# A two-layer graph network in seven-product form: small products of the unit matrix ahead of TensorE's work, new places for the first and last graphs, and a bank of its own for one seed of the last graph

## The chip, the cores and the metric

The kernel runs on one core of one Trainium2 chip. The metric is the device time of one execution in microseconds; the median of three runs is given. TensorE (PE, with its weight loads PEld), VectorE (DVE), ScalarE (ACT), GpSimd (POOL) and SyncE (SP) each work through a queue of their own in order; SP only issues transfers here.

## The reference

64 graphs of 256 nodes with 512 features pass through two layers. Each layer normalises the rows, applies a ReLU, and adds what a graph layer makes of them.

```
# layer 0
h   = max(layernorm(x), 0)
agg = adj @ h / max(rowsum(adj), 1e-6)
x   = x + relu(concat(h, agg) @ W.T)
# layer 1
h  = max(layernorm(x), 0)
Xw = h @ Wv + bv
e  = leaky_relu((Xw @ aw[:512])[None, :] + (Xw @ aw[512:])[:, None] + ab, 0.2)
T  = adj * exp(e);  T = T / (rowsum(T) + 1e-12)
H  = h @ Wk[0] + bk[0] + (T @ h) @ Wk[1] + bk[1] + (T @ T @ h) @ Wk[2] + bk[2]
x  = x + relu(H)
```

Everything is float32.

## The kernel before

**Stages.** Each graph goes through twelve stages: `loads`, `prepare` (the first normalisation, the scaled adjacency `an`, the turning of both), `prepared`, `wide` (h times the weights of layer 0, in 26 products of 128x128 by 128x256), `layer0` (the adjacency's part in seven such products, and `finish`, which adds the result to `x`), `turn1` (the second normalisation, to `h1n`, and the four dot products `z` on DVE that give `sj`), `transition` (T, turned to `tt`), `moved` (sums of blocks of T on the left side, `st`), `once` (T @ h, to `zg`), `inner` (times Wk[2], to `qf`), `turned1` (the load of the turned `h1n`), and `outer` (all three terms of H, and the output). Matrix products are split into 2x2 blocks and done with seven block products in place of eight. The sums of blocks that this needs are made on POOL (`pool_op`, L422; for the first and last graphs some go to DVE, L420), the evictions from PSUM by ACT (`copy`, L471) and DVE (`plus` and `minus`, L474 and L477; the wide stage's own at L652).

**Order.** No scheduler decides the order. Every operation is put down with `add(...)` under the name of its stage, and gets a time from a table: `AT[stage][n] + graph * 38.52`. `emit` sorts by this time, and each engine's queue is the sorted list of its own operations. The time only sets the order: an operation starts when its engine reaches it and its inputs are there. Graphs 0, 1, 2, 62 and 63 have tables of their own (`_0`, `_1`, `_2`, `_late`, `_last`), all others share one. A first table, `first`, and one named `weights` hold the loads and the making of the weights' forms.

**Places that matter below.**

- The transfers at the head are issued by SP in the order of the tables: the four tiles of W of layer 0 (`weights_l0`, L784, 512 KB each, which land in the buffers of `x[2]` to `x[5]`), `x[0]` in two halves (L904), then adjacencies, `x[1]`, and the weights of layer 1 (L828 to L840). At most eight are under way: the ninth waits for the first, and so on.
- `weights_l0` turns W on PE (L796, 32 transposes in eight banks); ACT copies and DVE sums (L812, L814) make 26 forms of it.
- `transition` sends `sj` to DRAM (L686, `ds`) and reads it back into all partitions as `row` (L687). ACT makes the leaky ReLU and the exponential from it, DVE multiplies with the adjacency (L697), ACT scales (L703) and, for graphs 0, 62 and 63, PE turns the result (`flip_on_pe`, L404), after which one copy on DVE and one on ACT (L410) make `tt`.
- `put` turns blocks on DVE (L376) and writes them to DRAM in four transfers (L380); `get` reads them back (L386). `turned1` gets `h1t` this way; POOL's sums for `outer` (`left_of_h`) wait for it.
- `main` works in three banks `p`, `r`, `d`: products 5, 1, 6 and 7 add up in `p`, and DVE takes the seeds of the others out of `p` between them; products 2 and 3 then add to the two halves of `r`, 4 to `d`. For graph 63 (`last` given) the seed of product 3 stays in the upper half of `r`, product 2 works on the lower half, and an ACT copy (L546) then moves the seed to the bank `y`, in which product 3 works. The copy waits for what uses bank `r`.

Of the kernel before, what the change touches and what calls it, by code (L numbers as in the profile page):

```python
# [11 lines left out]
AF = mybir.ActivationFunctionType  # L12
# [3 lines left out]
P = 128  # L16
# [8 lines left out]
WARM = 0  # L25
TURN = 38.52
AT = {
    "first": (-90.93, -53.23, -117.99, -108.94, -110.36, -116.23, -69.23, -51.75, -160.39, -107.21, -61.21, -22.37, -27.53, -12.34, -45.26, -1.78,
        -84.29, -28.27, -93.32, 13.37, -47.15, -20.43, -156.60, -71.50, -119.21, -46.84, -42.27, -129.45, -122.63, -61.71, -52.35, -32.94, -72.67,
        -62.56, -45.91, -151.57, -67.52, -60.72, 2.83, 15.02, -11.78, 19.40, 29.16, -47.95, -25.77, 48.23, -47.81, -32.81, -19.46, -48.89, 7.13,  # L30
        20.41, -32.63, 17.85, 10.53, -123.51, 5.76, 21.86),
    "inner": (105.13, 108.59, 106.23, 109.69, 109.89, 110.76, 112.05, 116.38, 111.97, 114.07, 117.47, 117.50, 122.79, 115.08, 117.06, 118.02, 137.51),
    "inner_0": (104.64, 107.10, 112.63, 109.63, 108.85, 109.21, 114.17, 115.99, 113.73, 110.41, 129.80, 114.72, 119.54, 110.75, 113.34, 116.02,
        129.11),
    "inner_1": (110.70, 112.22, 111.49, 112.47, 113.83, 115.31, 114.08, 115.66, 116.33, 115.18, 129.29, 117.74, 125.91, 116.89, 117.80, 117.56,
        155.03),
    "inner_2": (110.70, 111.20, 111.98, 113.63, 111.78, 114.32, 114.94, 116.88, 115.46, 116.06, 116.42, 116.98, 124.86, 117.74, 119.04, 117.57,
        134.35),
    "inner_last": (336.53, 367.29, 384.59, 334.45, 391.73, 454.67, 522.64, 533.37, 408.60, 470.37, 504.02, 528.93, 492.30, 558.54, 500.07, 537.12,
        580.23),  # L40
    "inner_late": (108.31, 111.76, 110.85, 113.85, 112.13, 112.69, 114.05, 114.68, 123.33, 115.61, 145.82, 118.27, 122.89, 115.88, 119.11, 120.04,
        164.89),
    "layer0": (20.96, 24.01, 34.26, 38.15, 36.30, 37.47, 38.90, 39.56, 40.20, 40.90, 41.49, 42.16, 41.93, 42.79, 43.22, 43.47, 44.25),
    "layer0_0": (43.30, 43.73, 40.76, 63.15, 62.04, 64.91, 63.69, 65.17, 65.45, 66.86, 68.03, 68.37, 68.31, 69.19, 69.32, 68.45, 68.75),
    "layer0_1": (31.27, 36.57, 33.97, 43.43, 46.13, 48.74, 46.62, 49.21, 46.86, 49.66, 48.01, 49.83, 48.25, 48.79, 50.67, 49.93, 50.78),
    "layer0_2": (24.88, 28.19, 23.22, 43.47, 37.98, 37.09, 39.47, 39.22, 40.19, 41.59, 40.57, 42.04, 42.75, 43.10, 41.23, 47.00, 44.33),
    "layer0_last": (50.01, 57.68, 33.91, 60.79, 65.66, 66.71, 68.41, 66.94, 69.01, 68.24, 69.91, 69.27, 70.80, 71.03, 72.73, 71.96, 75.23),
    "layer0_late": (15.20, 21.71, 35.30, 40.31, 42.84, 48.47, 47.89, 49.57, 47.98, 49.76, 48.90, 49.94, 48.91, 50.48, 49.70, 51.70, 50.97),
    "loads": (-59.49, -45.29),
    "loads_2": (-40.12, -36.06),  # L50
    "loads_last": (-58.91, -32.90),
    "loads_late": (-54.89, -85.13),
    "moved": (89.04, 92.46, 93.17, 93.66, 94.15, 98.50),
    "moved_0": (94.08, 96.00, 97.15, 96.58),
    "moved_1": (87.63, 93.34, 94.62, 96.56, 97.69, 105.10),
    "moved_2": (88.68, 91.56, 91.23, 91.84, 96.02, 106.19),
    "moved_last": (139.05, 163.46, 205.96, 169.91),
    "moved_late": (96.66, 97.72, 100.63, 101.15),
    "once": (61.25, 64.00, 75.09, 75.88, 94.29, 95.59, 94.96, 99.41, 98.19, 98.63, 100.80, 101.23, 101.56, 100.30, 105.75, 103.00, 102.97, 103.89,
        106.56, 107.35, 108.14),  # L60
    "once_0": (85.34, 86.38, 98.69, 87.50, 93.62, 98.46, 98.58, 97.73, 98.58, 100.34, 100.69, 102.20, 101.36, 98.56, 103.24, 103.33, 102.27, 102.98,
        104.33, 105.25, 108.42),
    "once_1": (57.59, 69.48, 97.24, 96.50, 95.31, 95.58, 95.01, 99.66, 97.26, 98.27, 100.29, 102.15, 100.46, 102.80, 103.34, 105.40, 106.15, 108.95,
        105.21, 110.88, 111.17),
    "once_2": (63.41, 76.25, 69.81, 96.68, 93.52, 97.13, 93.09, 100.30, 100.95, 102.43, 103.05, 103.30, 102.21, 102.90, 103.59, 109.13, 104.57,
        107.39, 107.54, 109.97, 115.46),
    "once_last": (102.80, 135.83, 148.28, 162.89, 124.41, 120.18, 145.98, 187.50, 162.35, 203.89, 212.10, 233.57, 187.89, 213.05, 223.02, 232.11,
        256.18, 243.42, 255.25, 267.18, 321.27),
    "once_late": (66.99, 88.23, 64.29, 90.92, 99.96, 101.37, 100.45, 101.19, 101.37, 101.90, 105.80, 107.13, 110.31, 103.81, 110.60, 107.37, 105.93,
        106.50, 106.70, 107.63, 115.35),  # L70
    "outer": (108.93, 110.52, 122.87, 129.37, 114.22, 117.68, 119.41, 120.07, 120.70, 121.57, 122.87, 123.53, 124.60, 125.46, 126.33, 126.99, 127.62,
        130.65, 131.52, 132.19, 128.92, 131.95, 134.55, 134.99, 141.93, 152.31, 138.02, 140.19, 162.69, 160.60, 164.14, 164.93),
    "outer_0": (94.35, 98.74, 125.62, 106.70, 102.31, 116.27, 117.12, 118.24, 117.50, 117.80, 121.31, 124.46, 124.00, 125.58, 126.52, 126.71, 128.22,
        128.87, 132.65, 133.67, 128.80, 131.21, 134.36, 137.61, 140.55, 144.44, 136.33, 141.49, 160.49, 160.36, 163.66, 166.03),
    "outer_1": (106.89, 111.90, 118.77, 120.53, 108.75, 117.68, 119.18, 119.21, 120.59, 120.95, 123.23, 122.93, 123.75, 126.63, 126.70, 127.43,
        127.87, 128.74, 130.19, 132.33, 130.44, 131.84, 139.05, 141.13, 148.79, 152.10, 133.45, 136.68, 160.29, 160.80, 164.22, 166.72),
    "outer_2": (108.39, 111.96, 127.91, 140.81, 108.40, 121.23, 123.19, 121.63, 124.71, 125.64, 126.27, 125.65, 128.28, 128.68, 129.01, 128.91,
        131.04, 134.92, 135.36, 134.36, 132.23, 135.69, 137.94, 142.17, 143.69, 152.32, 138.41, 140.22, 150.30, 161.80, 164.00, 171.57),
    "outer_last": (498.02, 668.57, 694.33, 671.17, 577.46, 581.61, 593.26, 565.87, 615.19, 623.17, 650.49, 630.60, 695.13, 726.44, 735.87, 784.68,
        743.01, 838.42, 843.34, 796.04, 842.17, 761.60, 792.50, 751.08, 788.70, 811.00, 818.37, 858.45, 840.44, 876.17, 953.80, 975.74, 975.14,  # L80
        1020.56, 876.63, 891.60, 907.44, 875.80, 872.80),
    "outer_late": (109.06, 117.31, 186.73, 151.51, 116.15, 116.30, 119.62, 120.47, 120.01, 120.90, 123.12, 123.38, 129.10, 132.52, 132.66, 129.78,
        134.77, 139.77, 140.44, 139.50, 141.87, 144.49, 145.13, 158.57, 188.07, 200.85, 150.49, 152.04, 158.47, 232.29, 199.18, 211.96),
    "prepare": (-43.06, -41.74, -40.72, -35.30, -36.24, -28.72, -27.19, -23.45, -19.80, -15.93, -24.36, -24.98, -20.94, -12.75, -1.76, -2.28, -14.82,
        -13.49, -12.68, -12.13, -11.03, -11.58, -0.32, 1.04, 0.48, 2.14, 1.59),
    "prepare_0": (-84.88, -53.30, -37.93, -28.72, -22.39, -78.13, -74.85, -6.63, -18.20, -7.49, -144.71, -60.68, -137.04, -101.76, -12.58, -21.22,
        -26.38, -2.11, -10.47, 18.05),
    "prepare_1": (-15.07, -17.62, -8.06, -6.13, -0.14, -1.19, -0.63, 0.54, 7.75, 18.63, -38.44, -18.61, -14.54, 4.73, 16.46, 7.28, 12.55, 17.02,
        21.02, 19.33),
    "prepare_2": (-29.75, -29.48, -28.24, -24.75, -27.62, -28.40, -18.19, -16.40, -14.88, -13.91, -13.33, -6.35, -3.17, 8.62, 7.51, 7.67, -7.58,  # L90
        -2.32, -3.08, -1.25, 10.97, -0.12, 9.45, 9.24, 6.13),
    "prepare_last": (-41.49, -47.42, -40.82, -36.74, -38.40, -39.37, -36.21, -27.41, -24.96, -22.93, -7.95, -5.29, -3.53, 0.52, -2.38, -0.41, -8.95,
        -8.06, 0.10, 9.16, 6.05, -3.83, 2.64, 1.68, 2.00, -1.88, -3.02),
    "prepare_late": (-34.61, -47.32, -24.01, -19.75, -22.44, -22.19, -20.22, -19.93, -12.10, -16.22, -28.31, -35.76, -26.99, -25.62, -0.63, -19.64,
        -11.10, -13.45, -13.43, -9.03, -11.19, -7.53, -0.35, -0.68, -1.43, -1.97, 0.33),
    "prepared": (-7.18, 5.89, 11.28),
    "prepared_0": (8.94, 11.22, 28.01, 44.28),
    "prepared_1": (30.89, 31.47, 31.46, 30.86),
    "prepared_2": (13.00, 25.59),
    "prepared_last": (9.25, 6.90, 2.69),  # L100
    "prepared_late": (-3.13, 0.63, 10.23),
    "transition": (52.39, 56.28, 64.51, 63.42, 65.05, 63.97, 66.52, 67.12, 67.73, 68.04, 68.40, 68.92, 69.51, 71.25, 71.80, 70.70, 72.35),
    "transition_0": (74.09, 74.94, 85.61, 86.74, 87.55, 87.22, 90.49, 90.24, 90.60, 91.41, 91.25, 92.03, 91.61, 91.53, 93.51, 94.10),
    "transition_1": (53.67, 62.32, 65.20, 65.85, 69.15, 70.70, 67.77, 67.85, 67.92, 69.48, 74.55, 74.24, 70.13, 70.67, 70.52, 71.81, 77.46),
# [5 lines left out]
    "turn1_1": (49.63, 49.70, 50.51, 51.10, 51.13, 51.73, 53.03, 53.21, 53.66, 53.93, 58.29, 58.86, 64.81, 54.56, 54.30, 58.29, 62.00, 58.02, 61.54),  # L110
    "turn1_2": (43.11, 45.01, 43.93, 52.82, 53.16, 53.50, 49.16, 51.40, 52.03, 52.20, 54.30, 57.90, 58.08, 51.29, 54.09, 59.58, 56.28, 52.52, 56.97),
    "turn1_last": (75.41, 78.96, 77.17, 178.47, 184.64, 192.21, 86.15, 103.27, 80.59, 81.84, 83.21, 85.38, 104.79, 93.44, 122.16, 115.84, 150.29,
        115.69, 113.30),
    "turn1_late": (42.12, 48.32, 51.63, 53.75, 53.93, 54.07, 55.81, 56.33, 52.09, 61.66, 67.71, 71.29, 74.60, 66.82, 79.34, 84.95, 89.16, 79.81,
        97.48),
    "turned1": (100.59,),
# [859 lines left out]
```

## Time and profile before

| | us |
|---|---|
| median of three runs (2547.05 to 2548.68) | 2547.44 |
| the profiled execution | 2545.75 |
| its span | 2544.0 |
| PE busy in the span | 2509.1 (99%) |
| POOL / DVE / ACT busy | 1560.1 / 1653.6 / 1322.6 |
| PE busy in the first 120 us | 95.3 |
| PE busy from 300 to 2300 us | 2000.0 |
| PE busy in the last 144 us | 134.2 |

All times of the profile are microseconds from the start of the span. One line of a timeline gives start, duration, engine, source line, operation, output and input by the names of the program, the number of instructions, and in brackets the idle time before it and what ended that. A product of 128x256 appears as two MATMUL records; at the full clock it takes 0.43 us, a transpose 0.11 us. The column PEclk of a table by stretches is the granted clock of TensorE, 1.00 for the full one. The ends of matmuls are modelled, so a stretch that shows PE busy throughout may hold short waits.

### The profile page before, as it was taken

How to read it: one execution, taken by the hardware profiler on the slowest of the kernel's cores; microseconds unless marked ns; L12 is line 12 of the kernel's file. 1: busy time of each engine (PE TensorE's matmuls, PEld its weight loads, DVE VectorE, ACT ScalarE, POOL GpSimd, SP SyncE). 2: the span in 40 equal slices, each digit the busy share in tenths (PEclk: the TensorE clock that was granted, in tenths of full speed). 3: DMA queues.
4: the chain of work that ended last, by engine and by line, in shares of the span. 5: the costliest groups of instructions: out<-in, count | busy, mean ns of one | idle time of the engine just before them, and what ended most of it. 6: DMA issues, size and time to landing. Idle time of an engine off the chain costs nothing.

```text
span 2544.0 us, 39950 instructions
## 1 busy us (share of the span) xinstructions
PE 2509.1 (99%) x12412; PEld 2213.5 (87%) x12412; DVE 1653.6 (65%) x4099; ACT 1322.6 (52%) x3551; POOL 1560.1 (61%) x2475
## 2 busy tenths in 40 slices
PE   7899999999999999999999999999999999999998
PEld 5688888888888888888888888888888888888887
DVE  5766666666666666666666666666666666666654
ACT  7455555555555555555555555555555555555521
POOL 5565666666666666666666656656666666666640
PEclk9999999999999999999999999999999999999999
DMA  4354454454454454444444544544544544544421
GB/s 150 85 131 117 113 129 120 115 125 117 117 129 112 115 135 110 119 125 120 120 120 116 127 121 111 128 122 113 127 119 117 126 113 116 135 112 115 110 71 44
DMA packets 574571, 296.85 MB, mean 117 GB/s; under 512 B 417171, under 2 KB 540819, under 8 KB 574358
## 3 DMA queue, kind: packets, MB, share of 16 engines
q1 hardware_dynamic: 574358, 294.31, 47.0%
q8 instruction: 98, 1.61, 0.3%
q14 instruction: 115, 0.94, 0.1%
HBM read 162.80 MB, written 131.40 MB: 116 GB/s over the span
## 4 chain that ended last, share of the span: by engine, by line
PE 96%; DVE 1%; DMA 1%; SPq 0%; ACT 0%; issue 0%; POOL 0%; DVEq 0%; ACTq 0%; POOLq 0%
PE bank L459 96%; DMA dh<-turned 0%; DMA x<-in_L_gnn_W_dram 0%; DMA l<-in_L_gnn_Wv_dram 0%; SPq L380 0%; DVE bank L474 0%; DVE zg L420 0%; DMA out_dram<-x 0%; DVE z L677 0%; DVE turned L376 0%; PE bank L404 0%; ACT h1n L362 0%; DVE bank L652 0%; SPq L345 0%; DVE zg L474 0%
## 5 line engine op out<-in xcount | busy, mean ns | idle before, releaser
L459 PE MATMUL bank<-l,s 128*128 128x256 f32 x3292 | 876.9, 380 | 6.6 <-ACT bank L546 2.1
L459 PEld LDWEIGHTS bank<-l,s 128*128 128x128 f32 x3292 | 611.6, 191 | 91.4 <-issue 5.1
L471 ACT COPY stg<-bank 128x256 f32<-128x256 f32 x944 | 337.2, 371 | 524.8 <-PE bank L459 203.6
L459 PE MATMUL bank<-l,zg 128*128 128x256 f32 x1820 | 469.2, 380 | 1.6 <-ACT mz L471 0.9
L459 PE MATMUL bank<-lq,zg 128*128 128x256 f32 x1792 | 447.8, 380 | 3.7 <-DVE zg L474 1.3
L459 PEld LDWEIGHTS bank<-lq,zg 128*128 128x128 f32 x1792 | 340.4, 190 | 51.1 <-DVE zg L474 2.3
L459 PEld LDWEIGHTS bank<-l,zg 128*128 128x128 f32 x1820 | 337.2, 191 | 42.3 <-ACT mz L471 1.7
L422 POOL TENSOR_TENSOR zg<-zg 128x256 f32<-128x256 f32 x183 | 131.7, 733 | 353.8 <-ACT zg L471 347.4
L652 DVE TENSOR_TENSOR bank<-bank,stg 128x256 f32<-128x256 f32 x505 | 210.3, 428 | 202.1 <-PE bank L459 138.8
L459 PE MATMUL bank<-l,h0t 128*128 128x256 f32 x1008 | 291.3, 382 | 1.6 <-DVE q L652 0.8
L422 POOL TENSOR_TENSOR s<-h0t,s 128x256 f32<-128x256 f32 x315 | 234.0, 743 | 0.5
L459 PEld LDWEIGHTS bank<-l,h0t 128*128 128x128 f32 x1008 | 197.4, 197 | 26.8 <-DVE q L652 2.3
L677 DVE SCALAR_TENSOR_TENSOR z<-h1n,v_sb 128x512 f32<-128x512 f32 x256 | 211.9, 828 | 13.1 <-ACT h1n L368 4.4
L459 PE MATMUL bank<-l,h1t 128*128 128x256 f32 x784 | 203.3, 381 | 1.3 <-DVE lo L477 1.0
L471 ACT COPY qf<-bank 128x256 f32<-128x256 f32 x128 | 47.6, 372 | 285.3 <-DVE qf L474 250.3
L422 POOL TENSOR_TENSOR qf<-qf 128x256 f32<-128x256 f32 x122 | 113.5, 930 | 117.4 <-DVE qf L474 117.4
L459 PEld LDWEIGHTS bank<-l,h1t 128*128 128x128 f32 x784 | 153.1, 197 | 20.1 <-DVE lo L477 2.3
L563 DVE SCALAR_TENSOR_TENSOR x<-bank,x 128x512 f32<-128x512 f32 x254 | 165.4, 686 | 2.7 <-PE bank L459 1.9
L459 PE MATMUL bank<-q,sa 128*128 128x256 f32 x512 | 152.9, 380 | 2.3 <-DVE bank L474 1.6
L459 PE MATMUL bank<-qf,st 128*128 128x256 f32 x512 | 152.6, 380 | 0.8 <-DVE qf L420 0.7
L422 POOL TENSOR_TENSOR s<-h0t 128x256 f32<-128x256 f32 x189 | 143.5, 773 | 9.3 <-ACT h0t L410 6.6
L422 POOL TENSOR_TENSOR hf<-h1n,hf 128x256 f32<-128x256 f32 x124 | 91.3, 736 | 89.9 <-PE bank L459 89.9
(178 smaller groups left out, 4418.3 us busy)
## 6 DMA issues: line engine op xcount, KB each, us to landing
dh<-turned SPq DMA_DIRECT2D x500, 128.0 KB, 3.3
h1t<-dh SPq DMA_DIRECT2D x64, 512.0 KB, 3.8
x<-in_x_dram SPq DMA_DIRECT2D x63, 512.0 KB, 4.6
out_dram<-x SPq DMA_DIRECT2D x63, 512.0 KB, 3.1
h0t<-dh SPq DMA_DIRECT2D x61, 512.0 KB, 4.0
a<-in_adj_dram SPq DMA_DIRECT2D x64, 256.0 KB, 4.3
dan<-turneda SPq DMA_DIRECT2D x248, 64.0 KB, 1.9
raw<-dan SPq DMA_DIRECT2D x62, 256.0 KB, 2.7
```

Source lines behind the costliest of these rows:

```text
L422: add("POOL", cost, lambda: getattr(nc.gpsimd, f)(to, p, q), reads, writes)
L459: nc.tensor.matmul(ps, lhs, rhs, start=start, stop=True, skip_group_check=True)
L471: add("ACT", 0.37, lambda: nc.scalar.copy(dst, bank[b][:, cols]), [f"bank{b}"], dkeys)
L563: add("DVE", 0.75 if sums else 0.69, lambda c=c: nc.vector.scalar_tensor_tensor(t[:, c, :], bank[banks[1 + c]], 0.0, t[:, c, :], op0=ALU.m ...
L652: add("DVE", 0.43, lambda f=f, to=to, x=x, y=y: getattr(nc.vector, f)(to, x, y), pbk + [k], tok)
L677: add("DVE", 0.79, lambda s=s, c=c: nc.vector.scalar_tensor_tensor(scr.rearrange("p c n -> p (c n)"), h[:, c, :], 1.0, v_sb[:, s, :], op0= ...
```

## The change

1. `WARM` goes from 0 to 7. `warm` is now called inside `first`, under a table of its own: 7 groups of four products of the unit matrix with itself (128x128 by 128x128) into bank 2, which nothing reads. Their times place five groups at the head of PE's queue, ahead of the first transposes of W, and two groups between the first 12 and the next 16 of these transposes. They need only `ident`, which POOL makes.
2. In `main`, for graph 63, the seed of product 3 goes into a bank of its own (bank 7, lower half) straight from `p`. The ACT copy between products 2 and 3 is gone; both work on different banks.
3. The tables of the first three and last two graphs, and those of `first` and `weights`, get new times. The tables of graphs 3 to 61 stay.
4. Three cost figures of `add` change (0.66 to 0.82, 0.74 to 0.91, 0.45 to 0.61); `emit` does not use them.

What the new times move on the queues, as far as it is spoken of below:

- SP: `x[1]` is loaded first, before W and `x[0]`; the adjacencies of graphs 0, 2 and 1 come right after W; `l_3` of layer 1 moves to the end of the weights (29th), `aw` from 14th to 23rd, the adjacency of graph 3 behind the first writes of the turned `h1n`. `row` of graph 0 stands directly behind its `ds` (before: behind one write of the turned `h1n`); `row` of graph 1 stands behind `ds`, one write of the turned `an`, the load of `h1t` and three writes (before: the load of `h1t`, the load of `x[4]` and four writes).
- PE: the first two products of `wide` for graph 0 stand ahead of the transposes of Wv (before: the first of them behind four of these). The transposes of T of graph 0 follow the last product of `layer0` of graph 1 directly.
- DVE: the products with the adjacency for T of graph 0 stand ahead of the two additions that finish `layer0` of graph 1 (before: behind them).
- ACT: at the head the sums and squares of `x[0]` come before most of the copies of W's forms.
- POOL: the sum that waits for `h1t` of graph 0 comes behind all of the sums of `once` of graph 0 (before: ahead of some). The sum of weights `l_7` stands ahead of the last two sums of `wide` of graph 0 and of the first of `layer0`'s four.
- At the tail, of the last `outer`: product 2 follows product 7 (before: it stands in the middle of it), then 4 and 3. The second of graph 63's dot products `z` stands behind one subtraction of `outer` of graph 62 (before: ahead of it).

```diff
-WARM = 0
+WARM = 7
 AT = {
+    "warm": (-428.00, -428.00, -428.00, -428.00, -428.00, -302.00, -302.00),
...
         p, r, d = banks[:3]
+        e, cols = (banks[4], lo) if last else (r, hi)
...
         step(6, p, lo, terms)
-        plus(bank[r][:, hi], [f"bank{r}"], p, lo, s12, keys[1:])
+        plus(bank[e][:, cols], [f"bank{e}"], p, lo, s12, keys[1:])
         step(7, p, lo, terms)
         if last:
-            x, y = banks[3:]
+            x = banks[3]
             plus(bank[x][:, lo], [f"bank{x}"], p, lo, s21[:, 1], keys[1:])
             last(1, hi, x, lo)
             plus(bank[d][:, lo], [f"bank{d}"], p, lo, s21[:, 0], keys[:1])
             step(2, r, lo, terms)
-            add("ACT", 0.37, lambda: nc.scalar.copy(bank[y][:, lo], bank[r][:, hi]), [f"bank{r}"], [f"bank{y}"])
             last(0, lo, r, lo)
-            step(3, y, lo, terms)
-            last(0, hi, y, lo)
+            step(3, e, cols, terms)
+            last(0, hi, e, cols)
             step(4, d, lo, terms)
             last(1, lo, d, lo)
...
+    def warm():
+
+        for _ in range(WARM):
+            def run():
+                for k in range(FC):
+                    nc.tensor.matmul(bank[2][:, k * P : (k + 1) * P], ident, ident, start=True, stop=True, skip_group_check=True)
+            add("PE", 0.86, run, ["ident"], ["bank2"])
+
     def first():
...
         add("ACT", 1.3, lambda: nc.scalar.copy(spare, mhalf), ["mhalf"], ["spare"])
+        kept = plan.count
+        plan.stage("warm")
+        warm()
+        plan.stage("first")
+        plan.count = kept
         weights_l0()
         load(0, "a")
         load(1, "x")
         load(1, "a")
```

## The prediction

> **What bounds the kernel now.** I read the page's busy shares first, then a table of stretches, then PE's timeline at both ends, and last what PE waits for there on the other queues.
>
> ```profile
> span 2544.0 us, 39950 instructions
> PE 2509.1 (99%) x12412; PEld 2213.5 (87%) x12412; DVE 1653.6 (65%) x4099; ACT 1322.6 (52%) x3551; POOL 1560.1 (61%) x2475
> ```
>
> PE bounds it. The stretches (length, then busy time and instructions of PE, PEld, DVE, ACT, POOL, then PEclk, DMA share, GB/s) say where PE is not at its best:
>
> ```profile
> 20.00:23.40 3.40, 3.40 (x13) 2.85 (x12) 2.66 (x6) 2.06 (x5) 3.24 (x5) 0.51 1.11 331
> 78.00:88.00 10.00, 6.31 (x21) 4.86 (x21) 8.01 (x21) 3.94 (x9) 1.68 (x3) 0.50 0.34 95
> 300.00:2300.00 2000.00, 2000.00 (x9971) 1782.36 (x9970) 1317.35 (x3272) 1064.02 (x2852) 1272.40 (x2024) 1.00 0.49 120
> ```
>
> The middle is full at the full clock. The change leaves its tables alone, and PE's work stays the same except for 28 small products, so everything is won or lost in the first 126 us and the last 20. In the first 120 us PE idles 120 − 95.3 = 24.7, and it runs at half clock until 23.4 and again from 78 to 88. PE's timeline at the head:
>
> ```profile
> 11.08 4.32 PE L796 MATMUL bank<-ident,x 128*128 128x128 f32 x19 [1.12 <-DMA x<-in_L_gnn_W_dram]
> ...
> 19.86 1.00 PE L459 MATMUL bank<-l,h0t 128*128 128x256 f32 x2
> ...
> 80.77 1.22 PE L459 MATMUL bank<-tt,h1n 128*128 128x128 f32 x4 [0.46 <-ACT tt L410]
> ...
> 94.00 1.13 PE L459 MATMUL bank<-lq,zg 128*128 128x256 f32 x4 [0.48 <-DVE zg L474]
> ```
>
> The landmarks of graph 0 are the first product of `wide` (19.86), `once` (80.77) and `inner` (94.00). Between `layer0` of graph 1 (last product about 73.6) and `inner`, PE mostly waits for graph 0's chain, because no other graph has work yet. On SP, DVE and POOL that chain reads:
>
> ```profile
> 57.78 0.35 SPq L686 DMA_DIRECT2D ds<-sj  x1
> 63.50 0.35 SPq L380 DMA_DIRECT2D dh<-turned  x1
> 63.94 0.44 SPq L687 DMA_DIRECT2D row<-ds  x1
> ```
>
> ```profile
> 74.41 0.42 DVE L697 SCALAR_TENSOR_TENSOR z<-z,a 128x256 f32<-128x256 f32 x1
> ```
>
> ```profile
> 89.22 0.84 POOL L422 TENSOR_TENSOR s<-h1t 128x256 f32<-128x256 f32 x1 [9.55 <-DMA h1t<-dh]
> ```
>
> SP sends `row` 6.2 us after `ds`, held behind one write that waits for DVE. DVE reaches the adjacency products at 74.41, though the exponential is ready at 70.6, because the additions at L563 stand ahead. POOL sits 9.55 us behind a sum that needs the turned `h1t`, with sums for `once` queued behind it. The tail, by the chain of waits and by PE's timeline:
>
> ```profile
> 2532.44 0.78 DVE bank L474 x2
> 2533.22 0.02 issue
> 2533.24 0.76 DVE x L756 x2
> ...
> 2534.08 0.37 ACT bank L546
> ```
>
> ```profile
> 2534.49 1.13 PE L459 MATMUL bank<-l,s 128*128 128x256 f32 x4 [2.09 <-ACT bank L546]
> 2535.46 1.82 PE L459 MATMUL bank<-l,h1t 128*128 128x256 f32 x4
> ```
>
> The copy waits for two DVE seeds and two evictions, PE idles 2.09, and the half clock follows: the last ten products (20 records) take 6.29.
>
> **The change part by part** (gains against the profiled 2545.75, which is 1.69 under the median of 2547.44).
>
> *Warm products.* None is in the trace. Records of 128x128 take 0.11 at the full clock (four in 0.45 from 88.53 to 88.98), and twice that at half. A product is two records, so 0.22 or 0.43. The first 20 can start when `ident` is ready, at 1.4 (after two POOL steps of 1.00 and 0.29). If the clock rises as it did before, 3.5 us into steady products (19.86 to 23.4), eight cost 0.43 and twelve 0.22: 3.5 + 2.6, to about 7.5; all at half, to 10.0. What covers this is the load of W. By the transposes' starts, 0.5 MB had landed at 4.35 and 2.75 MB at 11.03, so (11.03 − 4.35)/2.25 = 2.97 us a MB. With `x[1]` now first, W's second tile completes 1.75 MB in, about 8.1, and the group that waited until 11.08 now waits until 11.8 (3.0 MB). The last eight products (1.8) lie inside that wait. So nothing if the clock rises; without cover, 10.0 + 12 × 0.227 + 8 × 0.43 = 16.1 against 11.8, or 4.3 late.
>
> *A. First product of `wide`.* `x[0]`'s second half is 2.0 MB in, 8.8. ACT's sums and squares, now ahead of W's copies, end about 11.4; five small POOL steps take it to 13.0, the two normalisations on ACT to 15.5, and PE's turning with the copies (L410) to 17.15. The product starts at 17.2 instead of 19.86: 2.7. If the clock stays up, part of the 1.8 us lost before 23.4 (half of 3.54) comes back; I take 0.8, as the waits between would fill some of it. A = 3.5, bounds 0 (the loads set it anyway) and 4.5 (2.7 + 1.8).
>
> The row bearing on the clock is the one above: 19 transposes back to back from 11.08 to 15.40 took 4.32/19 = 0.227 each, the spacing of the half clock, and full speed came only 3.5 us after real products began. (PEclk reads 1.00 there, so I go by the spacing.) The Trainium skill, page "TensorE: Matmul & The Clock Gate", section "Part 4: PE-mode transpose", says that transposes don't count as work for the clock; with "Part 1: The HAM clock gate", where an idle window drops it again, the speed won by the warm products would be lost before 17.2, since only transposes lie between. By that rule A would be 2.7 and the sum below 12.6.
>
> *B. Start of `once`.* `row` directly behind `ds` goes out 2.9 after it (the time `ds` needs to be sent and land), 60.7 instead of 63.94: 3.2 earlier. The adjacency products no longer stand behind the additions, worth 3.8 (74.41 − 70.6). Then they end before PE is free, and PE sets the start: `layer0` of graph 1 ends 3.5 earlier, at 70.1, the four turns follow (0.4). The copies to `tt` then stand on ACT behind two evictions of 0.69, 0.2 of small work and two squares of 0.72: 70.5 + 1.4 + 0.2 + 1.4 − 0.4 overlapped + 0.27 = 73.4. `once` at 73.4 against 80.77 is 7.4 in all. Bounds 3.5 (A alone) and 9.5 (copies not held).
>
> *C. `once` to `inner`.* Now 13.2, of which 3.2 is half clock (6.31 busy in 78 to 88) and part POOL's sum for `h1t`; moved behind the sums of `once`, it no longer holds them. What remains is graph 1's chain, whose ACT and DVE work (two L570 0.8, two normalisations 1.45, copies and a normalisation 1.4, then `z` 0.7, turns 1.4, a difference 0.4) ends about 5.0 after `once` starts; four turned products and `zg` with its sums, at the durations of graph 0 before, take 4.6. So 9.6, and `inner` at 83.0: 11.0 in all. Bounds: 13.2 (nothing won) and 5.5 (graph 63's own distance, 2507.34 to 2512.80).
>
> *D. `inner` to graph 1's `once`.* PE idles 3.5 there now (32.0 long, 28.5 of work). Graph 0's sums for `outer` wait for `h1t`, whose DMAs (3.8 in the page's median, 7.6 at most) now start less early than PE arrives. I take −1.0, bounds +3.5 (all idle gone) and −5. The head gives 10.0.
>
> *E. The tail.* Without the copy, and with products 2, 4, 3 behind 7, product 2's 2.2 us cover the 1.2 of DVE seeds. The 2.1 of idle go, and so does the half clock: ten products at full clock take 4.35 + 0.16, so 1.8 more. Against it, graph 63's second `z` stands behind a subtraction of graph 62's `outer` (which waits for PE): about 1.5 late, while `an` was ready at 2504.98 and its turns began at 2505.61, so 0.6 of slack, and some 0.4 of work moved ahead of the turns. I count −0.5. E = 3.4, bounds 1.9 (clock not kept, second wait 0.2) and 4.0.
>
> The remaining moves (order of adjacencies, `aw`, `l_3`, `l_7`) lie before 60 us in transfers and POOL work that PE does not wait for in the trace of before; I cost them at nothing. `l_3` last of the weights would cost at most the 1.2 that PE waited for the first Wv tile, which lies in A's lower bound.
>
> Sum 10.0 + 3.4 = 13.4: profiled 2532.4, and with 1.7 the median **2534.0**.
>
> **The rivals.**
>
> *R1, half the head.* The waits move: `once` falls behind ACT's squares or graph 1's `z` (1.73 each on DVE), and C keeps its 13.2. Head 5.0, tail 3.4: 2539.0. For it: every chain step is a queue with other work in it. Against: three separate blocks are lifted.
>
> *R2, the head does not shorten.* DMA trips (2.9 for `ds`, 4.4 for `row`, `h1t` up to 7.6) set graph 0's chain, and what is won before 80 is waited for before 126. Only the tail: 2544.0, within 0.2%. For it: 9.55 on POOL is a DMA wait. Against: PE idles 3.5 at most after 94, so there is little to hide a loss in.
>
> *R3, slower.* The warm products don't raise the clock and hold PE to 16.1: W's groups are 4.3 late. SP's load of `x[2]` waits for PE's transposes out of that buffer, and the loads behind it in the queue are late too. A sparser PE then stays at half clock from 70 to 94: what ran at the full clock there (5.32 busy from 70 to 78, 4.91 from 88 to 94) takes 10.2 longer, of which 2.7 + 1.1 falls into PE's idle time of these stretches: 4.3 + 10.2 − 3.8 − 3.4 (tail) = +7.3, about 2554.7, the earlier `row` lost to the same late loads. It decides once the head is 8.5 later than before (the tail's 3.4 and 5.1 more). For it: 78 to 88 shows that the clock does fall in the head. Against: 28 full products are what raised it at 23.4.
>
> **How the numbers follow.** A run of this kernel tells 0.2% (5.1 us) from no change. Main case 0.62 (own range 2527 to 2538: C's lower bound gives 4 more, D's and B's bounds take 4), R1 0.20, R2 0.10, R3 0.08. The range 2527 to 2543 holds the main case and R1, and leaves R2, R3 and the main case's edges out. R2 lies within 0.2%: faster 0.82, same 0.10, slower 0.08.
>
> **What would show it.** The first records on PE are products of `ident`, at 0.22 a record, then 0.11 after about 5 us. `row` goes out some 3 us after `ds`. First product of `wide` at 17 to 18, `once` near 73, `inner` near 83; PEclk is near 1.00 between them. POOL has no 9 us wait ahead of `once`'s sums. At the tail, no ACT copy in the chain and ten last products in about 4.5. What breaks it: `once` at 80 or `inner` beyond 90 (R1, R2), the first W group after 13 (R3), or PE idle after `inner` growing by more than 5.

## The result: 0.28% slower, and the profile after

| | before | after |
|---|---|---|
| median of nine runs each, same chip | 2548.68 us (2547.05 to 2550.48) | 2555.06 us (2553.15 to 2558.05) |
| ratio to before, 95% interval | | 1.0028 (1.0019 to 1.0037) |
| span of the profiled execution | 2544.0 | 2553.3 |
| start of `once` / `inner` of graph 0 | 80.77 / 94.00 | 74.73 / 83.47 |
| output of graph 4 issued at | 311.92 | 304.49 |
| output of graph 56 issued at | 2315.15 | 2327.07 |
| from that output to the end of the span | 228.85 | 226.23 |

The forecast was 2534.0 us. The table says where to look: the head is 10.5 us earlier at `inner`, the tail is shorter, and between the outputs of graphs 4 and 56 a lead of 7.4 us turns into a lag of 11.9. The loss lies in the middle, whose tables the change does not touch.

The shares of the page of the changed kernel, and its stretches (columns as before: length, then busy time and instructions of PE, PEld, DVE, ACT and POOL, then PEclk, DMA share, GB/s):

```profile
span 2553.3 us, 40079 instructions
PE 2520.2 (99%) x12468; PEld 2212.0 (87%) x12468; DVE 1645.0 (64%) x4099; ACT 1322.9 (52%) x3550; POOL 1561.7 (61%) x2475
```

```profile
19.00:21.00 2.00, 2.00 (x11) 1.69 (x10) 2.00 (x7) 1.21 (x4) 0.35 (x1) 0.50 1.10 357
78.00:88.00 10.00, 9.13 (x51) 7.60 (x50) 5.89 (x17) 3.93 (x13) 5.60 (x7) 1.00 0.68 162
300.00:2300.00 2000.00, 1993.22 (x9877) 1762.81 (x9877) 1302.72 (x3239) 1056.91 (x2831) 1263.36 (x2008) 1.00 0.48 119
```

From 78 to 88 PE is busy at the full clock, where before it ran 6.31 us at half. From 300 to 2300 it is still 99.7% busy, but issues 9877 records in place of 9971. Such a share hides the loss, since the ends of matmuls are modelled; the count shows it, and so does the busy time of the weight loads, 1762.81 in place of 1782.36. The issue times of the outputs show it exactly: their distance is 38.52 us before (1005.36, 1043.88, 1082.40) and 38.89 after (1004.54, 1043.42, 1082.32). From graph 4 to 56 it is (2315.15 − 311.92)/52 = 38.524 against (2327.07 − 304.49)/52 = 38.896, so 0.372 us per graph on the mean.

The chain of waits of the changed kernel between 1000 and 1080, in order of time (start, us, what), has a gap in every graph; before, this stretch was a single piece of PE:

```profile
999.81 36.15 PE bank L461 x181
1035.96 0.13 issue
1036.08 38.76 PE bank L461 x192
1074.85 0.13 issue
```

Around that gap, VectorE, ScalarE and the weight loads of the changed kernel, from its timelines:

```profile
1035.17 0.42 DVE L476 TENSOR_TENSOR qf<-bank,qf 128x256 f32<-128x256 f32 x1 [0.58 <-ACT qf L473]
1035.52 0.42 DVE L476 TENSOR_TENSOR bank<-bank,p 128x256 f32<-128x256 f32 x1
```

```profile
1034.70 0.37 ACT L473 COPY qf<-bank 128x256 f32<-128x256 f32 x1 [3.73 <-PE bank L461]
```

```profile
1036.05 0.30 PEld L461 LDWEIGHTS bank<-q,sa 128*128 128x128 f32 x2 [0.50 <-issue]
```

And the same place before:

```profile
1035.59 0.42 DVE L474 TENSOR_TENSOR qf<-bank,qf 128x256 f32<-128x256 f32 x1 [0.18 <-PE bank L459]
1035.95 0.43 DVE L474 TENSOR_TENSOR bank<-bank,p 128x256 f32<-128x256 f32 x1
```

```profile
1036.05 0.37 ACT L471 COPY qf<-bank 128x256 f32<-128x256 f32 x1 [4.26 <-DVE qf L474]
```

The two operations belong to `inner`: `copy(*t3, bx, lo)` on ScalarE and `plus(*t2, bx, lo, *b11)` on VectorE. Both only read the half bank that the product put there. Before, VectorE goes first, as soon as PE is done, and ScalarE, which has time, waits for it. After, ScalarE goes first and VectorE waits for ScalarE: its idle time before t2 is 0.58 in place of 0.18, 0.40 more, about the 0.37 of the copy. Behind t2 stands the seed of `layer0` of a later graph (`bank<-bank,p`), and behind that PE.

No table moved these two. Their places on their own engines are the same in both kernels. What turned is the order in which the program is *built*. `emit` goes round the engines and lets each put down all that is ready, and the list of engines has the order in which they first appear among the sorted operations. The new times of the head (in the tables `prepare_0` and `first`) put ScalarE's first operation at −583.97 and VectorE's at −580.40 (before: −144.71 and −151.57), so the list is ACT, DVE, SP, POOL, PE, and was SP, PE, DVE, ACT, POOL. Of two operations on one bank, on two engines and with no other tie, the one that is built first goes first. The Trainium skill states the reason for any wait at all: page "PSUM — Partial Sum Buffer", section "PSUM bank collisions raise a hardware error", says that no two engines may touch one bank in the same partitions at once, two readers included. The rows agree (the copy ends at 1035.07, the sum starts at 1035.17); no run here shows what would happen if two engines were let in at once.

### The profile page after: what moved, and what is told of

Its sections match the earlier page's. It is cut to its first block, busy times and chain, and to the rows that moved or that the text cites. A ratio compares the mean times of both kernels' runs of the same rounds, so it can differ in the third digit from the quotient of the medians.

```text
span 2553.3 us, 40079 instructions
## 1 busy us (share of the span) xinstructions
PE 2520.2 (99%) x12468; PEld 2212.0 (87%) x12468; DVE 1645.0 (64%) x4099; ACT 1322.9 (52%) x3550; POOL 1561.7 (61%) x2475
## 4 chain that ended last, share of the span: by engine, by line
PE 95%; DVE 1%; DMA 1%; POOL 1%; issue 1%; ACT 1%; SPq 0%; DVEq 0%; POOLq 0%; ACTq 0%
PE bank L461 95%; DMA dtt<-turneda 0%; POOL s L424 0%; DMA x<-in_x_dram 0%; DMA raw<-dtt 0%; DMA dh<-turned 0%; PE bank L406 0%; DVE bank L476 0%; POOL q L424 0%; POOL sa L424 0%; ACT h1n L364 0%; DVE turneda L378 0%; ACT h1n L370 0%; POOL rstd L367 0%; DVE lo L479 0%
## 5 line engine op out<-in xcount | busy, mean ns | idle before, releaser
L424 POOL TENSOR_TENSOR s<-h0t 128x256 f32<-128x256 f32 x189 | 143.3, 774 | 13.4 <-ACT h0t L412 10.4
```

What stands on the lines that cost most here:

```text
L424: add("POOL", cost, lambda: getattr(nc.gpsimd, f)(to, p, q), reads, writes)
```

## The experiments

The first theory: the turned pair is the whole loss. Its rival: the middle is slower because TensorE starts it earlier, against the same loads and POOL sums. Ratios are to the kernel before on the same chip (its medians there: 2548.75 us for the first four, 2546.06 for the next four, 2548.13 for the last two).

| run | us | ratio (95%) |
|---|---|---|
| e1, old list of engines | 2536.43 | 0.9960 (0.9945 to 0.9975) |
| e2, before with the new list | 2568.28 | 1.0082 (1.0067 to 1.0097) |
| e3, one edge | 2534.81 | 0.9952 (0.9935 to 0.9969) |
| e4, tail alone | 2547.62 | 0.9994 (0.9985 to 1.0004) |
| e5, e3 without small products | 2532.99 | 0.9948 (0.9931 to 0.9964) |
| e6, e3 with POOL's sum early | 2541.78 | 0.9983 (0.9974 to 0.9993) |
| e7, e3 with T late | 2536.02 | 0.9960 (0.9945 to 0.9975) |
| e8, e3 with the gap filled | 2532.23 | 0.9947 (0.9932 to 0.9962) |
| e9, t2 behind the seed | 2546.23 | 0.9990 (0.9981 to 0.9999) |
| e10, edge in 30 graphs | 2545.36 | 0.9990 (0.9980 to 0.9999) |

**e1: the old list in the changed kernel.**

```diff
-        queues = {}
+        queues = {e: [] for e in ("SP", "PE", "DVE", "ACT", "POOL")}
```

> The changed kernel, with the list of engines from which the program is built put back to the order it has in the kernel before (SP, PE, DVE, ACT, POOL in place of ACT, DVE, SP, POOL, PE); every engine's own queue keeps its order. Theory 1 (ScalarE's copy t3 and VectorE's sum t2 of `inner` read the same bank; whichever is built first goes first, and after the change VectorE waits for ScalarE, 0.372 us in each graph of the middle): 59 graphs x 0.372 = 22 us come back, 2533 us (2530 to 2537). Theory 2 (the middle is slower because TensorE starts it earlier against loads and POOL): 2555 us, no change.

Measured 2536.43 us, 18.6 less than the changed kernel by the medians, with 38.52 us from output to output again. The first theory holds, the rival falls.

**e2: the new list in the kernel before.**

```diff
-        queues = {}
+        queues = {e: [] for e in ("ACT", "DVE", "SP", "POOL", "PE")}
```

> The kernel before, with the engines listed as in the changed kernel (ACT, DVE, SP, POOL, PE), nothing else. Theory 1: 0.372 us more in each of some 59 graphs, 2548.7 + 22 = 2570.6 us (2567 to 2574), with 38.9 us from output to output in the middle. Theory 2: 2548.7 us and 38.52 us from output to output.

2568.28 us, 19.5 more, and 38.89 from output to output (1012.78, 1051.67). One line, which moves no instruction on any engine, costs the old kernel 0.8%.

**e3: one edge.** The list stays as in the changed kernel; t3 is put behind t2 in graphs 3 to 61.

```diff
-        copy(*t3, bx, lo)
-        plus(*t2, bx, lo, *b11)
+        if 3 <= g < G - 2:
+            n = plan.count
+            plan.count = n + 1
+            plus(*t2, bx, lo, *b11)
+            plan.count = n
+            add("ACT", 0.37, lambda: nc.scalar.copy(t3[0], bank[bx][:, lo]), [f"bank{bx}"] + t2[1], t3[1])
+            plan.count = n + 2
+        else:
+            copy(*t3, bx, lo)
+            plus(*t2, bx, lo, *b11)
```

> The changed kernel with its own list of engines, but in graphs 3 to 61 the copy t3 is made to follow the sum t2 (one edge for each graph; head and tail keep every wait of the changed kernel). Theory 1 in its narrow form (this one pair is all of the loss): 2533 us, within 2 us of the run with the whole list put back. If other pairs matter: between 2535 and 2555 us. Theory 2: 2555 us.

2534.81 us: this pair alone is the loss in the middle. The times of e1 and e3 overlap, but their tails differ: from the output of graph 56 to the end it is 226.35 in e1 and 224.45 in e3 (224.6 in e6, e7 and e8 and 225.6 in e5, which have the tail of e3). In e1 the other pairs turn too, and PE waits at a place of the tail where none of those five has a wait; in e1's timeline:

```profile
2441.86 0.48 PE L461 MATMUL bank<-lq,zg 128*128 128x256 f32 x1 [0.92 <-POOL zg L424]
```

So the new tables of the tail fit the new list, and the shared tables fit the old one. For the head, these runs don't show which list fits.

**e4: the tail alone**, in the kernel before.

```diff
-WARM = 7
+WARM = 0
 AT = {
...
```

(The changed kernel's text, with every table but those named `_late` and `_last` from the kernel before; the list of engines is then the old one.)

> The kernel before with the tail of the change alone (the seed's own bank and the new places of the last two graphs; head, warm products and list of engines as before). The prediction's term E: 3.4 us less than before, 2545.3 us (bounds 1.9 to 4.0 us). By the difference of the two traces (9.3 us later at the end, 11.9 later at the output of graph 56): about 4 us less, 2544.7. If the tail's gain came from the head's earlier start: no gain, 2548.7.

2547.62 us, 1.1 less, and the interval takes in no change. In the traces its tail is 228.85 − 226.7 = 2.2 us shorter, against 4.4 in e3 (228.85 − 224.45). Part of the 2.2 between is a price of the old list: PE has the same wait of 0.92 in e4's trace as in e1's, at 2449.54. Where the rest goes isn't shown. The profiled head of e4 was itself 2.2 us later than that of before (output of graph 4 at 314.09) with the same tables: single profiles of the head scatter by this much and more (last section).

**e10: the edge in half of the graphs.**

```diff
-        if 3 <= g < G - 2:
+        if 3 <= g < 33:
```

> The one-edge kernel with its edge in graphs 3 to 32 alone (30 of 59). If the loss is a fixed price per graph: 0.372 us x 29 = 10.8 us more than with the edge in all, about 2545.6 us (0.9995 of the kernel before on the same chip), output distance 38.52 up to graph 31 and 38.89 after it. If the loss is a state of the whole pipeline, set once at the head: all of it or none.

2545.36 us, 2545.6 expected. Up to the output of graph 25 the distance is 38.52 (1074.09 to 1112.61), from that of graph 31 on 38.88 (1344.38 to 1383.26); single longer ones between them (two of 38.83) occur in other traces too. It is a fixed price per graph, not something set once at the head.

**e9: t2 behind the seed.** Here only a place in VectorE's queue moves, in the table of the middle graphs.

```diff
+_t = list(AT["inner"])
+_t[11] = 118.20
+AT["inner"] = tuple(_t)
```

> The changed kernel, its list of engines and its direction of the pair unchanged (ScalarE's copy t3 first, VectorE's sum t2 after it), but in the table that the middle graphs share t2 moves by one place on VectorE, behind the seed of layer0 that TensorE waits for. If the 0.372 us are the seed's wait behind t2 in VectorE's queue: the output distance is 38.52 again and the time 2533 to 2536 us as with the one edge (relative to the kernel before on the same chip, about 0.995). If t2 itself is what counts (the POOL sums and products that read it): still about 2555 us.

2546.23 us, between both expectations: the distance is 38.72, so 0.17 of the 0.372 came back and 0.20 stayed. Its timelines of VectorE, POOL, PE and PE's weight loads at the same place:

```profile
1034.59 0.43 DVE L479 TENSOR_TENSOR bank<-bank,p 128x256 f32<-128x256 f32 x1 [0.54 <-PE bank L464]
1034.93 0.41 DVE L479 TENSOR_TENSOR qf<-bank,qf 128x256 f32<-128x256 f32 x1
```

```profile
1035.43 0.73 POOL L427 TENSOR_TENSOR qf<-qf 128x256 f32<-128x256 f32 x1 [2.58 <-DVE qf L479]
```

```profile
1036.21 0.70 PE L464 MATMUL bank<-qf,st 128*128 128x256 f32 x2
```

```profile
1036.21 0.30 PEld L464 LDWEIGHTS bank<-qf,st 128*128 128x128 f32 x2 [0.33 <-POOL qf L427]
```

The seed no longer waits, but t2 ends at 1035.34, POOL's sum reads it and ends at 1036.16, and the product `qf,st` starts at 1036.21, right behind that sum, for which its weight load has waited 0.33. Two things waited for t2, one behind the other, and the second takes the place of the first.

The remaining four start from e3 and take up single terms of the prediction.

**e5: without the small products** (`WARM = 0`).

> The one-edge kernel (2534.8 us) without the 28 small products of the unit matrix; nothing else moves. The prediction's term A credits them with 0.8 us (the clock at the first products): 2535.6 us. If the transposes of W raise the clock themselves (in the kernel before the clock became full at about 16.5 with only transposes behind it), the transposes run at half clock a little longer and the first wide product comes 0 to 2 us later: 2535 to 2537 us. If the small products carry the head's gain (the clock low until past 20): first product beyond 19.5, once at 78 or later, 2539 us or more.

2532.99 us; by the ratios no difference from e3 (0.9948 and 0.9952). The first wide product starts at 17.48, against 17.24.

**e6: POOL's sum early.**

```diff
+_t = list(AT["outer_0"])
+_t[0] = 94.5
+AT["outer_0"] = tuple(_t)
```

> The one-edge kernel, with POOL's first sum for the outer product of graph 0 (which waits for the turned h1n to be loaded back) put ahead of the last sums for once, about where the kernel before has it. If the prediction's term C is right and reaches the end: POOL stands until about 84.5, the sums behind it end near 87 in place of 80.6, inner starts near 88 in place of 83, and about 5 us are lost: 2540 us. If what is won before inner is waited for later anyway (the second rival): 2535 us.

2541.78 us: 0.0031 of the ratio, about 8 us, is lost. POOL and PE in their timelines, and PE's clock over the stretch:

```profile
85.53 0.84 POOL L427 TENSOR_TENSOR s<-h1t 128x256 f32<-128x256 f32 x1 [9.55 <-DMA h1t<-dh]
```

```profile
87.79 1.23 PE L464 MATMUL bank<-tt,hf 128*128 128x128 f32 x4 [7.38 <-POOL hf L427]
```

```profile
80.00:96.00 16.00, 8.43 (x35) 6.79 (x35) 5.79 (x17) 4.36 (x13) 5.57 (x7) 0.79 0.47 126
```

One sum in the wrong place of POOL's queue stops PE for 7.38 us, and then the clock is at half for part of the stretch (mean 0.79), which the expectation of 5 us had left out. What is won before `inner` does reach the end, so the prediction's second rival, by which the head's gain is waited for later, falls.

**e7: T late.**

```diff
+_t = list(AT["transition_0"])
+_t[1] = 66.5
+_t[6:10] = [85.20, 85.21, 85.22, 85.23]
+AT["transition_0"] = tuple(_t)
```

> The one-edge kernel, with the products of T with the adjacency of graph 0 behind the two additions that finish layer0 of graph 1, and its row behind one write of the turned h1n, as in the kernel before. If the prediction's term B is right and reaches the end: the scaling of T comes 4 us later, once at 78.3 in place of 74.3, inner at 87, 2539 us. If it is hidden: 2535 us.

2536.02 us. In the trace `once` starts at 78.31 (74.32 in e3, so the 4.0 expected), `inner` at 86.70, and graph 4's output comes 3.85 later. Other profiles of the same head lie up to 4.8 later than e3 there too (last section), so PE's timeline says more than these differences: PE waits for the scaling of T where it has no wait in e3.

```profile
73.84 0.66 PE L410 MATMUL bank<-ident,an 128*128 128x128 f32 x2 [2.43 <-ACT an L709]
```

Behind it the clock is lower as well (PEclk 0.74 from 70 to 78 and 0.86 from 78 to 88; 1.00 in e3). Against e3 the time differs by 2 us (0.9960 against 0.9952), against e5 and e8 on its own chip by 3.0 and 3.8; all of these ratios lie inside each other's intervals. The mechanism is shown, its size at the end isn't.

**e8: the gap filled.** Two more groups of four small products, into bank 3, between W's last transposes and the first wide product.

```diff
+        plan.stage("warm2")
+        for _ in range(2):
...
+                    nc.tensor.matmul(bank[3][:, k * P : (k + 1) * P], ident, ident, start=True, stop=True, skip_group_check=True)
+            add("PE", 0.86, run, ["ident"], ["bank3"])
```

> The one-edge kernel with two more groups of four small products, in the 2.7 us in which TensorE waits between the last transposes of W and the first wide product (14.5 to 17.2). If the half clock from 18.8 to 22.2 in that run is the answer to this idle stretch: it goes, and the 3.4 us at half clock give back up to 1.7: 2533 us, first product still at about 17.2. If the clock falls for another reason: 2535 us and a half-clock stretch as before.

The stretches of e3, and then of e8:

```profile
14.40:17.20 2.80, 0.14 (x2) 0.00 (x0) 2.77 (x10) 2.80 (x9) 0.00 (x0) 1.00 0.84 289
18.00:23.00 5.00, 5.00 (x21) 3.71 (x22) 5.00 (x15) 4.45 (x14) 2.94 (x5) 0.66 1.11 316
```

```profile
14.40:17.20 2.80, 2.16 (x18) 1.91 (x17) 2.77 (x10) 2.80 (x9) 0.00 (x0) 1.00 0.91 294
18.00:23.00 5.00, 4.15 (x24) 2.94 (x24) 5.00 (x15) 4.62 (x15) 3.16 (x5) 1.00 1.03 306
```

The half clock is gone, so it was the answer to the idle stretch. Yet `inner` starts only 0.3 earlier (82.75 against 83.06, less than single profiles scatter) and the time is the same: from 18 to 23 VectorE is busy throughout with the forms of W, and PE, now faster, waits for it (4.15 busy in place of 5.00).

e3 and e8 are both faster than the kernel before and the changed one; at 0.9952 and 0.9947 they can't be told apart.

## Why the prediction was wrong

**The step that failed** is the sentence that set its frame: "The change leaves its tables alone, and PE's work stays the same except for 28 small products, so everything is won or lost in the first 126 us and the last 20." The tables of the middle were left alone, but not its waits. A term was put at nothing: 59 graphs by 0.372 = 21.9 us. e1, e2, e3 and e10 show it from four sides. Nearly all that the prediction named as its signs came true (the small products, `row`, the first wide product at 17.66, POOL, the tail), but all of them lie at the two ends; none looked at the middle.

**The sum without that term was good.** 13.4 us were predicted; e3, which takes out the term alone, is 13.9 us faster than before by the medians. By the changed kernel itself, 21.9 − 6.4 (2555.06 − 2548.68) = 15.5. That it came so close is partly luck: below, A and B are too large and E too small. The first rival, half the head, falls too: 13.9 is far from its 8.4.

**Its parts**, by the landmarks of the changed kernel. Each is read from one profile, and profiles of the same head differ by 2 us and more (last section), so the waits are firm, but misses of 1 or 2 us are not:

- *Warm products.* In PE's timeline the 40 records take 6.59, slow and then fast, as said:

```profile
1.35 6.59 PE L908 MATMUL bank<-ident 128*128 128x128 f32 x40 [1.35 <-POOL ident masks.py:199]
...
17.66 1.40 PE L461 MATMUL bank<-l,h0t 128*128 128x256 f32 x4 [2.69 <-DVE l L816]
...
74.73 0.61 PE L461 MATMUL bank<-tt,h1n 128*128 128x128 f32 x4
```

  They hold nothing up, and by e5 they bring nothing that can be measured.
- *A*, 3.5 predicted. The first wide product is 2.2 earlier (2.7 said) and the last product of `layer0` of graph 1 2.4 (70.66 against 73.06). The 0.8 for the clock was wrong: it fell again (0.50 from 19 to 21), and in e8, which keeps it up, only 0.3 is won by `inner`, since VectorE bounds that stretch.
- *B*, 7.4 predicted, 6.0 measured at `once`. Most of the missing 1.4 is A's. Directly behind `ds`, `row` went out 2.98 us after it (56.01 and 58.99; 2.9 said), and e7 shows the rest of the mechanism.
- *C*, 11.0 predicted with all before it, 10.5 measured at `inner`; from `once` it is 8.7 where 9.6 was said. POOL makes the sums of `once` before it waits for `h1t`, and then waits little:

```profile
79.14 1.54 POOL L424 TENSOR_TENSOR hf<-h1n,hf 128x256 f32<-128x256 f32 x2
...
85.11 0.84 POOL L424 TENSOR_TENSOR s<-h1t 128x256 f32<-128x256 f32 x1 [2.52 <-DMA h1t<-dh]
```

  e6 shows that the step is needed, and that it was worth more than the 3.6 in the sum: the lost clock comes on top.
- *D*, a loss of 1.0 predicted. At graph 1's `once` 7.9 are left, a loss of 2.6; with the one edge 9.1 are left there, and 9.6 at graph 4's output, against 10.0 predicted for the head.
- *E*, 3.4 predicted. 4.4 with the new list (e3) and 2.2 with the old one (e4) by the traces; e4's measured 1.1 is not clear of noise. The copy is out of the chain, and the last ten products run from 2545.39 to 2549.86, 4.5 us. The size of this term depended on the list of engines as well, at least by the wait of 0.92.

**The third rival** gave about 2554.7 us for slow loads and a clock that stays low. The time came out close to it, the mechanism did not occur: PEclk is 1.00 from 78 to 88, and `inner` is 10.5 earlier. A time that fits is no evidence for the cause; the landmarks decide.

## What to carry to other kernels

Two operations that only read the same bank on two engines still wait for each other, and without a tie between them the order of building decides which one waits: say it with an edge where one of them stands ahead of the bottleneck's input. Where a change to one part can alter the order of building, compare the waits of the whole program, not only the order of each queue; here a third of a microsecond in each of 59 graphs (21.9) outweighed all that was won at the ends (13.9). In a profile, count the instructions in a stretch or measure from output to output, since a busy share of 99% hides such a loss.

## What the runs showed of the hardware

**Transposes raised TensorE's clock.** In e5, which has no small products, nothing but transposes of W runs on PE before 13.7; its timeline:

```profile
8.10 3.01 PE L806 MATMUL bank<-ident,x 128*128 128x128 f32 x13 [8.10 <-DMA x<-in_L_gnn_W_dram]
11.29 1.86 PE L806 MATMUL bank<-ident,x 128*128 128x128 f32 x15 [0.18 <-DMA x<-in_L_gnn_W_dram]
```

The first 13 take 3.01/13 = 0.23 each, the next 15 take 1.86/15 = 0.12: about 3 us of transposes were enough. The prediction read the kernel before otherwise ("full speed came only 3.5 us after real products began"). But there too full speed came first with transposes alone: four of them from 17.48 take 0.66, as four do in e5 from 13.69 behind the fast ones, and PEclk is 0.99 from 17 to 20, ahead of the first product at 19.86; the half clock from 20 to 23.4 is a later fall. And the page that it cited, "TensorE: Matmul & The Clock Gate", section "Part 4: PE-mode transpose" of the Trainium skill, says that transposes don't count for the clock. On this chip these runs say that they do. What brought the clock down in e3 was the idle stretch behind them (e8).

**The half clock came in stretches of one length.** In the heads of these runs, read in windows of 0.1 us, its stretches last 3.4 (e3 from 18.7, before from 19.9), 6.8 (e6 from 84.6, e7 from 73.9) or 10.2 (before from 77.9), so one, two or three times 3.4. A wait that brings the clock down thus costs more than itself: each such stretch is up to 1.7 us of work at the full clock (though in e8 taking one away won nothing at the end).

**The head scatters.** e4's output of graph 4 came 2.2 us later than that of the kernel before, with the same tables there. In e5's profile the clock was also at half for part of the stretch from 38 to 43 (mean 0.66), which e3's doesn't show, and its graph 4's output came 2.4 us later than e3's, though the times of the two don't differ. PE was busy in all of that stretch (5.00 of 5.00), so no wait in it explains the clock; the cause stays open. e9, whose head has the tables and the list of e3, had the same stretch (0.66), and its output of graph 4 came 4.8 later (307.06 against 302.30), of which its own price in the graphs up to there is under 1. A single profile of the head is good to some 2 to 4 us, so terms below that need repeated times.
